# Turning x for layer 1: from TensorE transposes to VectorE blocks of 32 and 16 partition-moving DMAs

## The chip, the cores and the metric

The kernel runs on one core of one Trainium2 chip. The metric is the device time of one execution in microseconds (us); the value given for a kernel is the median of several executions. The profile quoted below comes from one profiled execution of the same program, whose span is 2288.5 us.

## What is computed

The reference puts a batch of 128 graphs, each with 128 nodes and 512 features, through four layers. Every layer adds its result to x and normalises each node's row. Cut to what matters here:

```python
x.shape == (128, 128, 512)                       # float32: graphs b, nodes n, features d
# layer 0
x = layernorm(x + (adj @ x) @ weight + bias)
# layer 1: the layer that the change touches
q, k, v = x @ Wq.T, x @ Wk.T, x @ Wv.T
rel = adj.T * (q @ k.T)                          # 128 x 128 for each graph
rel = rel / norm(rel, axis=2)
x = layernorm(x + rel @ v)
# layer 2: graph attention with softmax, then elu(h' + beta * h)
# layer 3: a maximum over nodes of relu(adj terms), with bias b
```

Layer 1 needs x with its features on the partitions (here called xT), because both the middle product x (Wq' Wk) and the product with Wv sum over features. x as layer 0 leaves it has the nodes on the partitions. Turning it, per graph, is a transpose of 128 nodes by 512 features: four squares of 128 by 128.

## The kernel before

All 128 graphs are taken in 32 groups of G = 4. The four layers of different groups are interleaved: every piece of work has a place in a table, the pieces are sorted by place, and each engine receives its instructions in that order. One group follows another every 28 places. A large product is not done as eight block products but as seven, with sums and differences of the left blocks formed ahead on GpSimd (`left_factors`) and of the results on VectorE and ScalarE (`product`). A half, for the left blocks, is two graphs.

```python
TABLE = dict(
    load=[-20], ..., stats0=row(14.4, 0.4), norm0=[16.2], apply0=row(16.8, 0.33),
    turn=row(21.4, 1), x_sums=row(25.3, 0.5), m=row(28, 1, 7), scores=row(36.5, 1),
    ..., v=row(42, 1, 7), attend=row(50.6, 1), ..., store=[108.5])

def turn(b):                                     # once for each of the 4 graphs of a group
    if b == 0:
        s["xT"] = work.tile([P, K, G * P], FP, tag="aT_x", name=f"xT_{g}")   # one buffer only
    p = bank(f"p_xT_{g}_{b}")                    # a PSUM bank
    for k in range(K):                           # K = 4
        pe.transpose(p[:, k * P : (k + 1) * P], x1[g][:, b, k * P : (k + 1) * P], ident)
    act.copy(s["xT"][:, :, b * P : (b + 1) * P], p.rearrange("p (k n) -> p k n", k=K))

# left_factors: four GpSimd operations that read xT and write s_x
pool.tensor_tensor(s1, blk(1, 0), blk(1, 1), ALU.add)        # and three more of this kind

def by_columns(p, a, b, first):                  # the middle product, r_m: xT or s_x is moving
    for c in range(2):
        for k in range(2):
            pe.matmul(p[:, c, :], b[:, k, c * P : (c + 1) * P], a[:, k, :], ...)

def by_rows(p, a, b, first):                     # the product with Wv, r_v: xT or s_x is stationary
    for j in range(2):
        for k in range(2):
            pe.matmul(p[:, j, :], a[:, k, j * P : (j + 1) * P], b[:, k, :], ...)

def scores(b):                                   # p_rel: xT is stationary
    for k in range(K):
        pe.matmul(s["p"][:, b * P : (b + 1) * P], s["xT"][:, k, b * P : (b + 1) * P],
                  s["tT"][:, k, b * P : (b + 1) * P], ...)
...                                              # (cut)
```

Loads of x and stores of the result are issued from SyncE.

Of the kernel before, what the change touches and what calls it, by code (L numbers as in the profile page):

```python
# [8 lines left out]
FP = mybir.dt.float32  # L9
# [20 lines left out]
def kernel(  # L30
# [31 lines left out]

    nc = tc.nc
    pe, dve, act, pool = (InOrder(tc, e) for e in (nc.tensor, nc.vector, nc.scalar, nc.gpsimd))
    B, N, D = x.shape
    P = 128
    assert N == P and D % P == 0
    K = D // P
    H = D // 2
    G = 4  # L70
    NG = B // G
# [20 lines left out]
    def load(g):  # L92
        x1[g] = data.tile([P, G, D], FP, tag="x1", name=f"x1_{g}", bufs=3)
        if g == 0:
            for b in range(G):
                nc.sync.dma_start(x1[g][:, b, :], x[b])
        else:
            nc.sync.dma_start(x1[g], x[g * G : (g + 1) * G].rearrange("b n d -> n b d"))

    load(0)  # L100
    w0_sb = const.tile([P, K, D], FP)
# [124 lines left out]
    def row(at, step, n=G):  # L226
# [3 lines left out]
    TABLE = dict(  # L230
        load=[-20], y=row(0.5, 1), bias=row(1.3, 1), y_sums=row(5.2, 0.5), y_w=row(7, 1, 7),
        stats0=row(14.4, 0.4), norm0=[16.2], apply0=row(16.8, 0.33),
        turn=row(21.4, 1), x_sums=row(25.3, 0.5), m=row(28, 1, 7), scores=row(36.5, 1),
        masked=[39.95], norms=[42.5], inverse=[43.1], v=row(42, 1, 7), attend=row(50.6, 1),
        residual=row(51.0, 1), dots=row(54.2, 1.1), norm1=[55.2], scale=[58.8],
        apply1=row(65.4, 0.33),
# [5 lines left out]
        stats3=[99.8, 101.1, 104.7, 105.7], norm3=[106.2], apply3=row(107, 0.33), store=[108.5],  # L242
    )

    FIRST = {1: dict(y=row(-9.5, 0.3), bias=row(-9.2, 0.3))}

    LAST = {
        NG - 3: dict(
# [42 lines left out]
    def left_factors(at, s, aT, tag, name, keep):  # L291

        def blk(nh, kh):
            return s[aT][:, 2 * kh : 2 * kh + 2, 2 * P * nh : 2 * P * (nh + 1)]

        def first():
            sums = work.tile([P, 3 + keep, 2, 2 * P], FP, tag=tag, name=f"s_{name}")
            s1, s2, s4 = (sums[:, i] for i in range(3))  # L300
            s3 = sums[:, 3] if keep else blk(1, 0)
            s["f"] = {1: blk(0, 0), 2: blk(0, 1), 3: s4, 4: blk(1, 1), 5: s1, 6: s2, 7: s3}
            pool.tensor_tensor(s1, blk(1, 0), blk(1, 1), ALU.add)

        emit(at[0], first)
        emit(at[1], lambda: pool.tensor_tensor(s["f"][6], s["f"][5], blk(0, 0), ALU.subtract))
        emit(at[2], lambda: pool.tensor_tensor(s["f"][7], blk(0, 0), blk(1, 0), ALU.subtract))
        emit(at[3], lambda: pool.tensor_tensor(s["f"][3], blk(0, 1), s["f"][6], ALU.subtract))

    def by_rows(p, a, b, first):  # L310

        for j in range(2):
            for k in range(2):
                pe.matmul(
                    p[:, j, :],
                    a[:, k, j * P : (j + 1) * P],
                    b[:, k, :],
                    start=(first and j == 0 and k == 0),
                    stop=(j == 1 and k == 1),
                    skip_group_check=True,  # L320
                )

    def by_columns(p, a, b, first):

        for c in range(2):
            for k in range(2):
                pe.matmul(
                    p[:, c, :],
                    b[:, k, c * P : (c + 1) * P],
                    a[:, k, :],  # L330
                    start=(first and c == 0 and k == 0),
                    stop=(c == 1 and k == 1),
                    skip_group_check=True,
                )
# [103 lines left out]
    def layer1(g, t):  # L438
        s = {}

        def turn(b):
            if b == 0:
                s["xT"] = work.tile([P, K, G * P], FP, tag="aT_x", name=f"xT_{g}")
            p = bank(f"p_xT_{g}_{b}")
            for k in range(K):
                pe.transpose(
                    p[:, k * P : (k + 1) * P], x1[g][:, b, k * P : (k + 1) * P], ident
                )
            act.copy(
                s["xT"][:, :, b * P : (b + 1) * P], p.rearrange("p (k n) -> p k n", k=K)  # L450
            )

        def begin_middle():
            s["tT"] = work.tile([P, K, G * P], FP, tag="nat", name=f"tT_{g}", bufs=3)

        def begin_values():
            s["v"] = work.tile([P, G, D], FP, tag="nat", name=f"v_{g}", bufs=3)

        def middle_block(nh, ch):
            return s["tT"][:, 2 * ch : 2 * ch + 2, 2 * P * nh : 2 * P * (nh + 1)]  # L460

        def scores(b):
            if b == 0:
                s["p"] = bank(f"p_rel_{g}")
            for k in range(K):
                pe.matmul(
                    s["p"][:, b * P : (b + 1) * P],
                    s["xT"][:, k, b * P : (b + 1) * P],
                    s["tT"][:, k, b * P : (b + 1) * P],
                    start=(k == 0),  # L470
                    stop=(k == K - 1),
                )

        def masked():
            s["rel"] = work.tile([P, G, P], FP, tag="rel", name=f"rel_{g}", bufs=2)
            dve.tensor_tensor(
                s["rel"], s["p"].rearrange("p (b n) -> p b n", b=G), adj_b, ALU.mult
            )
            s["sq"] = work.tile([P, G, P], FP, tag="sq", name=f"sq_{g}")
            pool.tensor_tensor(s["sq"], s["rel"], s["rel"], ALU.mult)  # L480

        def norms():
            p = bank(f"p_n_{g}")
            for b in range(G):
                pe.matmul(p[:, b : b + 1], s["sq"][:, b, :], ones, start=True, stop=True)
            s["p"] = p

        def inverse():
            n2 = small.tile([P, G], FP, tag="n2", name=f"n2_{g}")
            dve.tensor_copy(n2, s["p"][:, :G])  # L490
            s["rn"] = small.tile([P, G], FP, tag="rn", name=f"rn_{g}")
            pool.tensor_tensor(s["rn"], n2, mhalf, ALU.pow)

        def attend(b):
            s["o", b] = bank(f"p_o1_{g}_{b}")
            pe.matmul(s["o", b], s["rel"][:, b, :], s["v"][:, b, :], start=True, stop=True)

        def residual(b):
            if b == 0:
                x2[g] = data.tile([P, G, D], FP, tag="x2", name=f"x2_{g}")  # L500
            dve.scalar_tensor_tensor(
                x2[g][:, b, :],
                s["o", b],
                s["rn"][:, b : b + 1],
                x1[g][:, b, :],
                op0=ALU.mult,
                op1=ALU.add,
            )
            stats(s, f"1_{g}", b, x2[g][:, b, :])


        def dots(b):
            if b == 0:
                s["d"] = small.tile([P, 2, G], FP, tag="d12", name=f"d12_{g}")
            for i in range(2):
                scr = work.tile([P, D], FP, tag="scr", name=f"scr_{g}_{b}_{i}", bufs=2)
                dve.scalar_tensor_tensor(
                    scr,
                    x2[g][:, b, :],
                    1.0,  # L520
                    wa[:, i, :],
                    op0=ALU.mult,
                    op1=ALU.mult,
                    accum_out=s["d"][:, i, b : b + 1],
                )

        def scale_dots():
            for i in range(2):
                dve.scalar_tensor_tensor(
                    s["d"][:, i, :],  # L530
                    s["mv"][:, :, 0],
                    wa_sum[:, i : i + 1],
                    s["d"][:, i, :],
                    op0=ALU.mult,
                    op1=ALU.add,
                )
            dve.tensor_tensor(
                s["d"], s["d"], s["r", 0][:, None, :].to_broadcast([P, 2, G]), ALU.mult
            )
            s12[g] = s["d"]  # L540

        each(t["turn"], turn)
        left_factors(t["x_sums"], s, "xT", "s_x", f"x_{g}", 1)
        product(t["m"], f"m_{g}", by_columns, s, "m", middle_block, True, begin_middle)
        each(t["scores"], scores)
        emit(t["masked"][0], masked)
        emit(t["norms"][0], norms)
        emit(t["inverse"][0], inverse)
        product(t["v"], f"v_{g}", by_rows, s, "v", rows_of(lambda: s["v"]), True, begin_values)
        each(t["attend"], attend)  # L550
        each(t["residual"], residual)
        each(t["dots"], dots)
        emit(t["scale"][0], scale_dots)
        norm(t["norm1"], t["apply1"], s, f"1_{g}", lambda: x2[g])
# [139 lines left out]
    def layer3(g, t):  # L694
        s = {}
# [12 lines left out]

        def store(i):
            for b in range(i * n, i * n + n):  # L710
                nc.sync.dma_start(out[g * G + b], x3[g][:, b, :])

        n = G // len(t["store"])
        each(t["widen"], widen)
# [46 lines left out]
```

## Time and profile before

| what | value |
|---|---|
| time, median of 3 | 2290.54 us (2290.47 to 2291.78) |
| span of the profiled execution | 2288.5 us |
| granted TensorE clock, mean | 0.996 |
| VectorE (DVE) busy | 1577.0 us, 69% |
| ScalarE (ACT) busy | 1005.3 us, 44% |
| GpSimd (POOL) busy | 959.2 us, 42% |
| moved by DMA in all | 75.21 MB |

How to read the profile: PE is TensorE's matmuls (a transpose is one of them), PEld its weight loads, which run beside matmuls. The names in a group, such as `p_xT<-ident,x`, are the tile that is written and the tiles that are read, in the program's names. Nearly all instructions are recorded at line 26, a helper, so that groups are told apart by tiles and not by lines. The chain of work that ended last is followed back from the last instruction, at each step to what released it or to the instruction ahead of it on its engine.

### The profile page before, as it was taken

The numbers are of one execution on the slowest core, as the hardware profiler recorded it, in microseconds if no ns is written. First come the engines' busy times: TensorE is split into PE (matmuls) and PEld (weight loads), VectorE is DVE, ScalarE is ACT, GpSimd is POOL, SyncE is SP. The second block draws the span as 40 slices with busy tenths as digits, with TensorE's granted clock in tenths as the row PEclk, the third lists the DMA queues.
The fourth block names the chain that finished last, engine by engine and source line by source line (L and its number), as shares of the span: only waits on it lengthen the run. The fifth ranks groups of instructions, "written<-read, shape, count | busy, mean of one in ns | idle before, by whom it ended". The sixth has DMA issues, their size and how long they took to land.

```text
span 2288.5 us, 31182 instructions
## 1 busy us (share of the span) xinstructions
PE 2250.7 (98%) x11809; PEld 1914.8 (84%) x11809; DVE 1577.0 (69%) x3319; ACT 1005.3 (44%) x1800; POOL 959.2 (42%) x775
## 2 busy tenths in 40 slices
PE   7999999999999999999999999999999999999996
PEld 5888888888888888888888888888888888888873
DVE  4656776666776667766667766667767677666677
ACT  2224444444444454444444444444444544444435
POOL 4434444344444334444344443444443344443422
PEclk9999999999999999999999999999999999999998
DMA  4000011100111100111100111001111001110001
GB/s 162 19 19 10 28 38 38 37 21 18 38 37 37 38 19 19 38 37 38 37 10 28 38 37 37 21 18 38 37 37 38 19 20 37 37 38 19 9 12 55
DMA packets 38886, 75.21 MB, mean 33 GB/s; under 512 B 3024, under 2 KB 3152, under 8 KB 38736
## 3 DMA queue, kind: packets, MB, share of 16 engines
q1 hardware_dynamic: 37536, 70.86, 8.7%
q10 hardware_dynamic: 1200, 2.36, 0.3%
q8 instruction: 93, 1.52, 0.3%
q14 instruction: 57, 0.47, 0.1%
HBM read 39.65 MB, written 33.55 MB: 32 GB/s over the span
## 4 chain that ended last, share of the span: by engine, by line
PE 94%; DVE 4%; POOL 1%; ACT 1%; issue 1%; DMA 0%; ACTq 0%; DVEq 0%; POOLq 0%
PE r_y L26 17%; PE r_v L26 16%; PE r_m L26 16%; PE r_z L26 16%; PE p_z L26 5%; PE p_rel L26 5%; PE p_o L26 5%; PE p_a L26 5%; PE p_y L26 5%; PE p_xT L26 2%; DVE x L26 1%; PE p_n L26 1%; DVE st L26 1%; PE p_eT L26 1%; PE p_m L26 1%; PE p_s L26 1%
## 5 line engine op out<-in xcount | busy, mean ns | idle before, releaser
L26 ACT ACTIVATE x<-x,nmean,rstd 128x512 f32<-128x512 f32 x512 | 386.4, 809 | 128.0 <-DVE nmean L26 127.9
L26 DVE BATCH_NORM_STATS2 st<-x 128x6 f32<-128x512 f32 x512 | 352.4, 688 | 75.3 <-ACT x L26 66.6
L26 POOL TENSOR_TENSOR rstd<-ve,mhalf 128x4 f32<-128x4 f32 (+1 forms) x134 | 144.5, 1078 | 245.3 <-DVE ve L26 241.3
L26 POOL TENSOR_TENSOR x<-x,bias_sb 128x512 f32<-128x512 f32 x128 | 174.8, 1368 | 145.5 <-PE p_y L26 145.5
L26 DVE SCALAR_TENSOR_TENSOR scr<-x,wa 128x512 f32<-128x512 f32 x256 | 214.9, 891 | 0.0
L26 ACT ACTIVATE x<-x,top 128x512 f32<-128x512 f32 x128 | 92.4, 722 | 254.1 <-DVE top L26 189.7
L26 DVE TENSOR_TENSOR x<-r_y,x 128x512 f32<-128x512 f32 x224 | 152.9, 683 | 54.4 <-PE r_y L26 44.5
L26 DVE TENSOR_TENSOR v<-r_v,v 128x512 f32<-128x512 f32 x96 | 65.8, 685 | 177.0 <-PE r_v L26 174.0
L26 POOL TENSOR_TENSOR s_x<-xT 128x512 f32<-128x512 f32 x64 | 82.2, 1285 | 222.2 <-ACT xT L26 222.2
L26 ACT COPY yT<-p_y 128x512 f32<-128x512 f32 x128 | 75.0, 586 | 206.0 <-PE p_y L26 206.0
L26 DVE SCALAR_TENSOR_TENSOR x<-p_o,rn,x 128x512 f32<-128x512 f32 x128 | 95.9, 749 | 99.5 <-PE p_o L26 96.5
L26 DVE SCALAR_TENSOR_TENSOR x<-m,x 128x512 f32<-128x512 f32 x128 | 115.1, 899 | 61.7 <-ACT m L26 51.3
L26 ACT COPY c<-r_z 128x512 f32<-128x512 f32 x124 | 72.6, 585 | 175.9 <-DVE scr L26 151.5
L26 PEld LDWEIGHTS p_y<-adjT,x 128*128 128x128 f32 x1024 | 135.3, 194 | 12.9 <-ACT adjT L26 5.0
L26 PEld LDWEIGHTS p_z<-eT,x 128*128 128x128 f32 x1024 | 135.4, 194 | 8.3 <-DVE x L26 1.2
L26 PE MATMUL p_y<-adjT,x 128*128 128x128 f32 x1024 | 136.1, 278 | 6.2 <-ACT adjT L26 4.7
L26 PEld LDWEIGHTS p_rel<-tT,xT 128*128 128x128 f32 x1024 | 134.2, 192 | 7.4 <-DVE tT L26 0.8
L26 PE MATMUL p_a<-x,adjT 128*128 128x512 f32 x256 | 133.6, 607 | 3.5 <-DVE mx L26 1.8
L26 PE MATMUL p_z<-eT,x 128*128 128x128 f32 x1024 | 136.4, 277 | 0.4 <-DVE x L26 0.4
L26 PE MATMUL p_rel<-tT,xT 128*128 128x128 f32 x1024 | 135.0, 275 | 0.6 <-DVE tT L26 0.6
L26 POOL TENSOR_TENSOR s_z<-zT 128x512 f32<-128x512 f32 x31 | 39.2, 1265 | 223.9 <-ACT zT L26 223.9
L26 PE MATMUL p_o<-v,rel 128*128 128x512 f32 x256 | 130.6, 594 | 0.0
(120 smaller groups left out, 5075.2 us busy)
## 6 DMA issues: line engine op xcount, KB each, us to landing
out_dram<-x SPq DMA_DIRECT2D x128, 256.0 KB, 2.0
x<-in_x_dram SPq DMA_DIRECT2D x31, 1024.0 KB, 5.2
w_sb<-in_L_gnn_weight_dram ACTq DMA_DIRECT2D x1, 1024.0 KB, 5.7
x<-in_x_dram SPq DMA_DIRECT2D x4, 256.0 KB, 7.5
wq_sb<-in_L_gnn_Wq_dram SPq DMA_DIRECT2D x1, 1024.0 KB, 11.7
wk_sb<-in_L_gnn_Wk_dram SPq DMA_DIRECT2D x1, 1024.0 KB, 14.6
w_sb<-in_L_gnn_W_dram ACTq DMA_DIRECT2D x1, 1024.0 KB, 10.2
wv_sb<-in_L_gnn_Wv_dram SPq DMA_DIRECT2D x1, 1024.0 KB, 13.7
```

What stands on the lines that cost most here:

```text
L26: return lambda *args, **kw: self.tc.keep_in_program_order(op(*args, **kw))
```

## The change

The transposes of x for layer 1 leave TensorE, and the copies out of PSUM leave ScalarE, for every group but the first. VectorE turns x in square blocks of 32 by 32 (one instruction for each graph). A block so turned lies on the 32 partitions from which it was read, so 16 DMAs for each group, issued from SyncE, then carry the blocks between the four sets of 32 partitions: one DMA for each pair of source set a and destination set q. Each carries 32 partitions by 8 runs by 64 elements of 4 bytes: 64 KB in runs of 256 bytes. So that a run is 256 bytes long and not 128, the columns of the two graphs of a half are interleaved: even columns belong to one, odd columns to the other. Matmuls that read xT or s_x as one graph therefore read every second element. The purpose is to give TensorE's time for the transposes to matmuls. Loads and stores on SyncE are now recorded in program order with the new DMAs.

```diff
@@ the table @@
-        turn=row(21.4, 1), x_sums=row(25.3, 0.5), m=row(28, 1, 7), scores=row(36.5, 1),
+        turn=row(18.4, 0.6), move=row(20.5, 0.1), x_sums=row(25.3, 0.5), m=row(28, 1, 7), scores=row(36.5, 1),
@@ columns of the two graphs of a half @@
+    def graphs(a, mixed):
+        if mixed:
+            return a.rearrange("p k (n j) -> p k j n", j=2)
+        return a.rearrange("p k (j n) -> p k j n", j=2)
@@ by_rows, for v alone with mixed=True @@
-                    a[:, k, j * P : (j + 1) * P],
+                    graphs(a, mixed)[:, k, j, :],
@@ by_columns @@
-                    p[:, c, :],
+                    p[:, c, :].rearrange("p (j n) -> p j n", j=2),
                     b[:, k, c * P : (c + 1) * P],
-                    a[:, k, :],
+                    graphs(a, True)[:, k, :, :],
@@ layer 1 @@
         def turn(b):
             if b == 0:
-                s["xT"] = work.tile([P, K, G * P], FP, tag="aT_x", name=f"xT_{g}")
-            p = bank(f"p_xT_{g}_{b}")
...
+                s["xB"] = work.tile([P, 2, K, Q, 2 * P // Q], FP, tag="xB", name=f"xB_{g}")
+                s["xT"] = work.tile([P, 2, K, 2 * P], FP, tag="aT_x", name=f"xT_{g}")
+            if g == 0:
...                                  (the first group: as before, with the columns interleaved)
+                return
+            dve.transpose(
+                s["xB"][:, b // 2].rearrange("p k q (u j) -> p (k q) u j", j=2)[:, :, :, b % 2],
+                x1[g][:, b, :].rearrange("p (c u) -> p c u", u=P // Q),
+            )
+
+        def move(a):
+            n = P // Q
+            for q in range(Q):
+                sync.dma_start(
+                    s["xT"][q * n : (q + 1) * n, :, :, 2 * a * n : 2 * (a + 1) * n].rearrange(
+                        "p h k n -> p (h k) n"
+                    ),
+                    s["xB"][a * n : (a + 1) * n, :, :, q, :].rearrange("p h k n -> p (h k) n"),
+                )
@@ scores @@
-                    s["xT"][:, k, b * P : (b + 1) * P],
+                    graphs(s["xT"][:, b // 2], True)[:, k, b % 2, :],
@@ the pieces of layer 1 @@
         each(t["turn"], turn)
+        if g > 0:
+            each(t["move"], move)
```

More of the change, by code (lines that the diff above doesn't have):

```diff
@@ L64 @@
     pe, dve, act, pool = (InOrder(tc, e) for e in (nc.tensor, nc.vector, nc.scalar, nc.gpsimd))
+    sync = InOrder(tc, nc.sync)
     B, N, D = x.shape
@@ L68 @@
     K = D // P
+    Q = P // 32
     H = D // 2
@@ L97, in load @@
         else:
-            nc.sync.dma_start(x1[g], x[g * G : (g + 1) * G].rearrange("b n d -> n b d"))
+            sync.dma_start(x1[g], x[g * G : (g + 1) * G].rearrange("b n d -> n b d"))
     load(0)
@@ L243 @@
     )
-    FIRST = {1: dict(y=row(-9.5, 0.3), bias=row(-9.2, 0.3))}
+    FIRST = {
+        0: dict(turn=row(20.4, 0.3)),
+        1: dict(y=row(-9.5, 0.3), bias=row(-9.2, 0.3))}
     LAST = {
@@ L295, in blk @@
         def blk(nh, kh):
+            if keep:
+                return s[aT][:, nh, 2 * kh : 2 * kh + 2, :]
             return s[aT][:, 2 * kh : 2 * kh + 2, 2 * P * nh : 2 * P * (nh + 1)]
@@ L308, in left_factors, with by_rows @@
         emit(at[3], lambda: pool.tensor_tensor(s["f"][3], blk(0, 1), s["f"][6], ALU.subtract))
-    def by_rows(p, a, b, first):
+    def graphs(a, mixed):
+        if mixed:
+            return a.rearrange("p k (n j) -> p k j n", j=2)
+        return a.rearrange("p k (j n) -> p k j n", j=2)
+    def by_rows(p, a, b, first, mixed=False):
         for j in range(2):
@@ L321, in by_rows, with by_mixed_rows @@
                 )
+    def by_mixed_rows(p, a, b, first):
+        by_rows(p, a, b, first, mixed=True)
     def by_columns(p, a, b, first):
@@ L442, in turn @@
             if b == 0:
-                s["xT"] = work.tile([P, K, G * P], FP, tag="aT_x", name=f"xT_{g}")
-            p = bank(f"p_xT_{g}_{b}")
-            for k in range(K):
-                pe.transpose(
-                    p[:, k * P : (k + 1) * P], x1[g][:, b, k * P : (k + 1) * P], ident
-                )
-            act.copy(
-                s["xT"][:, :, b * P : (b + 1) * P], p.rearrange("p (k n) -> p k n", k=K)
-            )
+                s["xB"] = work.tile([P, 2, K, Q, 2 * P // Q], FP, tag="xB", name=f"xB_{g}")
+                s["xT"] = work.tile([P, 2, K, 2 * P], FP, tag="aT_x", name=f"xT_{g}")
+            if g == 0:
+                p = bank(f"p_xT_{g}_{b}")
+                for k in range(K):
+                    pe.transpose(
+                        p[:, k * P : (k + 1) * P], x1[g][:, b, k * P : (k + 1) * P], ident
+                    )
+                act.copy(
+                    graphs(s["xT"][:, b // 2], True)[:, :, b % 2, :],
+                    p.rearrange("p (k n) -> p k n", k=K),
+                )
+                return
+            dve.transpose(
+                s["xB"][:, b // 2].rearrange("p k q (u j) -> p (k q) u j", j=2)[:, :, :, b % 2],
+                x1[g][:, b, :].rearrange("p (c u) -> p c u", u=P // Q),
+            )
+        def move(a):
[7 more added lines that the diff above has]
+                )
         def begin_middle():
@@ L548, in layer1 @@
         emit(t["inverse"][0], inverse)
-        product(t["v"], f"v_{g}", by_rows, s, "v", rows_of(lambda: s["v"]), True, begin_values)
+        product(t["v"], f"v_{g}", by_mixed_rows, s, "v", rows_of(lambda: s["v"]), True, begin_values)
         each(t["attend"], attend)
@@ L710, in store @@
             for b in range(i * n, i * n + n):
-                nc.sync.dma_start(out[g * G + b], x3[g][:, b, :])
+                sync.dma_start(out[g * G + b], x3[g][:, b, :])
         n = G // len(t["store"])
```

## The prediction

> **What bounds the kernel now.** I read the busy shares first, then the chain of work that ended last, then that chain inside one group, and last the waits and DMA issues around xT. The page's first part and the head of its chain:
>
> ```profile
> PE 2250.7 (98%) x11809; PEld 1914.8 (84%) x11809; DVE 1577.0 (69%) x3319; ACT 1005.3 (44%) x1800; POOL 959.2 (42%) x775
> ...
> PE 94%; DVE 4%; POOL 1%; ACT 1%; issue 1%; DMA 0%; ACTq 0%; DVEq 0%; POOLq 0%
> PE r_y L26 17%; PE r_v L26 16%; PE r_m L26 16%; PE r_z L26 16%; PE p_z L26 5%; PE p_rel L26 5%; PE p_o L26 5%; PE p_a L26 5%; PE p_y L26 5%; PE p_xT L26 2%; DVE x L26 1%; PE p_n L26 1%; DVE st L26 1%; PE p_eT L26 1%; PE p_m L26 1%; PE p_s L26 1%
> ```
>
> TensorE is busy 98% of the span and is 94% of the chain. A busy PE alone proves little, but its idle time is at most 2288.5 - 2250.7 = 38 us in all, so time can only be gained by giving it less to do. The transposes of x, p_xT, stand in the chain with 2%. What one costs there is read from the chain in one group's stretch (start, length, what):
>
> ```profile
> 1051.75 1.73 PE r_v L26 x8
> 1053.47 0.86 PE p_a L26 x2
> 1054.33 1.73 PE r_z L26 x8
> 1056.06 0.44 PE p_xT L26 x4
> 1056.49 1.73 PE r_z L26 x8
> 1058.22 0.44 PE p_xT L26 x4
> ...
> 1071.61 1.73 PE r_m L26 x8
> ```
>
> Pieces stand end to end without a gap, and the four transposes of a graph take 0.44 us of it. The group table says 273 ns for one such matmul, but they overlap; the 0.44 is what they hold up. The busy time of stretches of 4 us (stretch, its length, then busy PE, PEld, DVE, ACT and POOL) gives the room beside them:
>
> ```profile
> 1044.00:1048.00 4.00, 4.00 (x24) 3.64 (x23) 0.51 (x2) 4.00 (x8) 0.00 (x0) 1.00 0.00 0
> 1048.00:1052.00 4.00, 4.00 (x22) 3.26 (x21) 1.60 (x3) 1.40 (x3) 2.06 (x2) 1.00 0.00 0
> 1052.00:1056.00 4.00, 4.00 (x18) 3.10 (x17) 2.36 (x6) 1.80 (x3) 2.93 (x3) 1.00 0.02 4
> ```
>
> Here, where the change puts VectorE's transposes, TensorE is full and VectorE nearly free. Groups that give sizes for the new work, one wait, and the DMA issues:
>
> ```profile
> L26 PE MATMUL p_xT<-ident,x 128*128 128x128 f32 x512 | 76.2, 273 | 0.0
> L26 ACT COPY xT<-p_xT 128x512 f32<-128x512 f32 x128 | 74.5, 586 | 95.4 <-PE p_xT L26 95.3
> L26 DVE TENSOR_TENSOR x<-r_y,x 128x512 f32<-128x512 f32 x224 | 152.9, 683 | 54.4 <-PE r_y L26 44.5 <-POOL x L26 6.9 <-DVE nmean L26 0.3
> ```
>
> ```profile
> POOL s_x L26 <- ACT xT L26: 222.2, 31, 10.9
> ```
>
> ```profile
> out_dram<-x SPq DMA_DIRECT2D x128, 256.0 KB, 2.0
> x<-in_x_dram SPq DMA_DIRECT2D x31, 1024.0 KB, 5.2
> ```
>
> GpSimd waits 222 us for xT without holding anybody up, so xT may come somewhat earlier or later. A 256 KB store lands 2.0 us after its issue.
>
> [...]
>
> **Removed.** For 31 groups, 4 graphs each, four transposes on TensorE: 1.75 us a group (5.0% of the 35 us of the chain's stretch; 4 x 0.44). All of it lies in the full stretch of TensorE, so 31 x 1.75 = 54 us leave the path. ScalarE loses 124 copies of 0.586 us = 73 us, worth nothing on the path. Group 0 keeps its transposes.
>
> **Added on VectorE.** 124 transposes, estimated at 0.69 us from the 683 ns of a 128x512 operation: 86 us, which brings VectorE to 1663 us, 74% of a span of 2236. The built order puts them among the additions of r_v, at 1046 to 1053 in the time of the group above. Between 1044 and 1052 VectorE is busy 2.1 of 8 us, so 4 x 0.69 = 2.8 us fit. ScalarE's normalisation of x for the fourth graph ends near 1049, so the inputs are there, and the last transpose, behind the maximum of a p_a in the order, ends near 1053. Nothing on the path.
>
> **Added on the DMA queues.** 16 moves of 64 KB a group, 31 x 16 = 496 in all, 32.5 MB of 256-byte runs. xT has one buffer, so the first move waits for the last reader of the group ahead, the r_v piece that ends at 1053.47. From there to the first r_m at 1071.61 are 18.1 us, and 18.1 - 1.75 = 16.4 us after the change. A SyncE issue takes 0.33 us for a store and 0.39 us for a load in the trace's timeline. I choose 0.4: 16 x 0.4 = 6.4 us, and 2.0 us to land, so xT is whole 8.4 us after 1053.47, some 8 us before TensorE wants it. GpSimd needs 2 x 1.28 = 2.6 us for the first two sums, which TensorE wants at its third r_m step, 5.2 us into the product. That is in time too; xT even comes near 1062, earlier than the 1065 of the trace. [...]
>
> **Moved.** Stores of an older group now stand behind the moves in the queue and go out some us later; the next load, 8 us behind them, has most of a group's 69 us to spare. On TensorE the order is the old one without p_xT, and without the p_xT banks the p_o and p_y tiles turn over the four PSUM banks with fewer pieces between. VectorE reads a p_o within some 1.6 us, so a bank is free in time.
>
> **Sum.** 2290.5 - 54 = 2236; I add 1 us for small waits at the group borders and say 2237.
>
> **Rivals.** (1) *Strided operands.* All seven steps of r_m stream every second element, and the weight loads of r_v and p_rel read so. If strided reading were slower by only a tenth on r_m, 7 x 1.73 x 0.1 = 1.2 us a group, or 37 us, would go back, and the time would be near 2273. Weight loads have less room: a r_v load takes 190 ns beside a matmul that holds TensorE 216 ns (1.73/8). [...] for it nothing in the trace. (2) *The moves become the wait.* If one cost over 16.4/16 = 1.0 us, TensorE would wait at each r_m. At 1.2 us, 16 x 1.2 + 1 = 20.2 us, a wait of 3.8 us takes the place of 1.75 saved: 31 x 2 us more, near 2355. The trace's issues of 0.3 to 0.4 us and its 2.0 us landings speak against it[...]. (3) *VectorE.* From 1068 to 1076 it is busy 7.8 of 8 us; TensorE now gets there 1.75 us sooner a group. If VectorE's additions came late there, up to half of the gain is lost, near 2263. Against it: by the same view it is idle for 6.3 of the 16 us ahead of 1068, so it reaches that stretch sooner too.
>
> **Range and chances.** The gain of 54 us is the firmest number, and nothing in the profile can make it larger than the small waits that vanish with it, so the low end is close: 2230. The high end, 2275, holds the strided rival at a tenth and the VectorE rival. To be faster by over 2% the time must be under 2245, that is, only 9 us of the 54, 0.3 us a group, may be lost. I give 0.69 to faster, 0.23 to within 2% (rivals 1 and 3), and 0.08 to slower (rival 2).
>
> **What would show it.** Right: no p_xT in the chain beyond group 0; groups 67.7 us apart instead of 69.5; r_m pieces still 1.73 us and r_v loads still near 190 ns; a transpose on VectorE near 0.7 us; xT landed some 8 us ahead of the first r_m; TensorE's busy time down by about 54 us with idle time still near 38 us. Wrong: longer r_m, r_v or p_rel pieces (rival 1); TensorE waiting on a DMA for xT (rival 2); TensorE waiting on VectorE for tT, c or x (rival 3).

## The result and the profile after

| | time, median | runs |
|---|---|---|
| before | 2291.16 us | 2290.47 to 2291.84 |
| after | 2276.24 us | 2274.21 to 2276.67 |

The ratio is 0.9933, with a 95% interval of 0.9916 to 0.995. The change gains 15 us where the prediction had 54; the time lies just above the range of 2230 to 2275. The profile of after, busy time and the head of the chain of work that ended last:

```profile
PE 2226.3 (98%) x11313; PEld 1879.1 (83%) x11313; DVE 1763.1 (78%) x3443; ACT 939.2 (41%) x1676; POOL 1011.9 (44%) x775
...
PE 91%; DVE 5%; POOL 1%; issue 1%; ACT 1%; DMA 0%; SPq 0%; ACTq 0%; DVEq 0%; POOLq 0%
PE r_y L26 17%; PE r_v L26 16%; PE r_m L26 16%; PE r_z L26 16%; PE p_rel L26 5%; PE p_z L26 5%; PE p_o L26 5%; PE p_a L26 5%; PE p_y L26 4%; DVE x L26 1%; DVE scr L26 1%; PE p_n L26 1%; DVE st L26 1%; PE p_eT L26 1%; PE p_m L26 1%
```

p_xT has left the chain, as meant. But TensorE's busy time fell by 24 us and not by 54, and idle time rose from 38 to 48 us (2274.3 - 2226.3): TensorE does its remaining work more slowly, and waits more. VectorE's busy time grew by 186 us, of which the new transposes are only 84. In the names, r_y and r_z are the large products of layers 0 and 2, p_o is rel @ v, p_s and p_eT are small transposes of layer 2, and scr are VectorE's dot products of x with the attention weights of layer 2. The chain of after through the stretch shown in the prediction, and on to the product r_y:

```profile
1052.35 1.73 PE r_v L26 x8
...
1067.00 3.45 PE r_z L26 x16
1070.46 1.81 PE r_m L26 x8
1072.27 0.89 PE p_y L26 x8
...
1090.59 0.93 PE p_rel L26 x8
1091.52 1.96 PE r_y L26 x8
```

The last two pieces had these lengths before:

```profile
1091.16 0.89 PE p_rel L26 x8
1092.05 1.73 PE r_y L26 x8
```

A step of r_v still takes 1.73 us and p_y 0.89. A step of r_m now takes 1.81 instead of 1.73, and the p_rel of a graph 0.93 instead of 0.89. The r_y behind it takes 1.96 where nothing in it is strided: 0.23 us of that is a wait.

To say where all of the time went I took from the trace, for every TensorE matmul, the time from its start to the start of the next one, and added these up by the tile written. A wait counts with the piece ahead of it. The differences from before, in us:

| | p_xT | r_m | p_rel | p_o | p_s and p_eT | r_y | rest | sum |
|---|---|---|---|---|---|---|---|---|
| after | -54.1 | +18.5 | +7.1 | +8.8 | +5.2 | +1.7 | -1.4 | -14.2 |

So the 54 us were gained, and 40 us were given back: 41.3 in the columns from r_m to r_y, less 1.4 in the rest. A typical r_m matmul starts its successor after 227 ns instead of 216, a p_rel matmul after 118 instead of 112. The +8.8 at p_o is one wait, in group 1, from the list of TensorE's waits:

```profile
PE r_m L26 <- DMA xT<-xB: 8.8, 1, 8.8
```

The rest are small waits on VectorE, and most groups have none. Between the first r_m matmuls of groups 2 to 31 there are 29 distances. In after 21 of them are 68.47 or 68.48 us; the other eight are 69.04 to 70.61, together 9.4 us longer. In seven of the eight, GpSimd's first sum of xT starts only 2.0 to 3.1 us ahead of the first r_m matmul, because one of the 16 copies was issued or landed later than usual (why is not shown); in the 21 it starts 3.2 to 4.1 us ahead. The eighth follows two of the seven, and it is the one in the chain above.

Four reasons were to be tested, with the letters that the expectations use. A: the strided reading of xT and s_x slows TensorE by itself. B: the moves or VectorE's transposes slow r_m. C: xT is whole later than foreseen, so that GpSimd's sums of xT fall beside VectorE's operations and both are slowed. D: VectorE's 124 added transposes make it late by their own time. D is the rival of C, since both make TensorE wait on VectorE. Group 1's wait was to be removed by itself.

What speaks for C: the queue of SyncE in one group, and then GpSimd (the first line is before, the others after) and VectorE (after) beside the start of r_m (start, length, what; in brackets the idle time ahead of it and what ended it).

```profile
1054.14 10.40 SPq L26 DMA_DIRECT2D xT<-xB  x16
1064.64 2.01 SPq L26 DMA_DIRECT2D out_dram<-x  x4
```

```profile
1065.41 1.28 POOL L26 TENSOR_TENSOR s_x<-xT 128x512 f32<-128x512 f32 x1 [7.00 <-ACT xT L26]
...
1066.41 1.27 POOL L26 TENSOR_TENSOR s_x<-xT 128x512 f32<-128x512 f32 x1 [7.39 <-PE r_z L26]
...
1070.66 1.73 POOL L26 TENSOR_TENSOR s_x<-xT,s_x 128x512 f32<-128x512 f32 x1
```

```profile
1068.66 0.92 DVE L26 SCALAR_TENSOR_TENSOR scr<-x,wa 128x512 f32<-128x512 f32 x1
...
1069.51 1.75 DVE L26 SCALAR_TENSOR_TENSOR scr<-x,wa 128x512 f32<-128x512 f32 x1
...
1072.34 0.68 DVE L26 SCALAR_TENSOR_TENSOR scr<-x,wa 128x512 f32<-128x512 f32 x1
```

The group of scr, before and then after:

```profile
L26 DVE SCALAR_TENSOR_TENSOR scr<-x,wa 128x512 f32<-128x512 f32 x256 | 214.9, 891 | 0.0
L26 DVE SCALAR_TENSOR_TENSOR scr<-x,wa 128x512 f32<-128x512 f32 x256 | 274.6, 1124 | 0.0
```

Sixteen issues take 10.4 us, 0.65 from one to the next (median of an issue alone 0.61), and with 2.1 us to land xT is whole 12.3 us after its last reader. GpSimd's first sum shows the moment: 1066.41 (the bracket names PE r_z, but the last of the 16 copies lands at 1066.08, just ahead of it). That is 4.05 us ahead of the first r_m at 1070.46. Before the change it was 6.20 us ahead (1065.41 and 1071.61). The four sums therefore end 1.9 us after r_m begins instead of 1.1 us before, and lie beside VectorE's scr operations. One of these takes 0.68 us with no sum beside it and 1.75 beside one; the sum takes 1.73 instead of 1.27. Over the whole trace 111 of the 256 scr operations take more than 1 us, against 65 before: 51 lie beside a sum (31 before) and 58 beside the additions of the bias that GpSimd does after the sums (32 before). Of VectorE's 186 us more, 60 are scr's and 84 the transposes.

### The profile page after: what moved, and what is told of

It is laid out like the page before. It is cut to its first block, busy times and chain, and to the rows that moved or that the text cites. A ratio compares the mean times of both kernels' runs of the same rounds, so it can differ in the third digit from the quotient of the medians.

```text
span 2274.3 us, 31117 instructions
## 1 busy us (share of the span) xinstructions
PE 2226.3 (98%) x11313; PEld 1879.1 (83%) x11313; DVE 1763.1 (78%) x3443; ACT 939.2 (41%) x1676; POOL 1011.9 (44%) x775
## 4 chain that ended last, share of the span: by engine, by line
PE 91%; DVE 5%; POOL 1%; issue 1%; ACT 1%; DMA 0%; SPq 0%; ACTq 0%; DVEq 0%; POOLq 0%
PE r_y L26 17%; PE r_v L26 16%; PE r_m L26 16%; PE r_z L26 16%; PE p_rel L26 5%; PE p_z L26 5%; PE p_o L26 5%; PE p_a L26 5%; PE p_y L26 4%; DVE x L26 1%; DVE scr L26 1%; PE p_n L26 1%; DVE st L26 1%; PE p_eT L26 1%; PE p_m L26 1%
## 5 line engine op out<-in xcount | busy, mean ns | idle before, releaser
L26 DVE SCALAR_TENSOR_TENSOR scr<-x,wa 128x512 f32<-128x512 f32 x256 | 274.6, 1124 | 0.0
L26 POOL TENSOR_TENSOR x<-x,bias_sb 128x512 f32<-128x512 f32 x128 | 192.9, 1513 | 99.2 <-PE p_y L26 99.1
L26 POOL TENSOR_TENSOR s_x<-xT 128x512 f32<-128x512 f32 x64 | 95.7, 1495 | 253.6 <-PE r_z L26 124.5
L26 PEld LDWEIGHTS p_rel<-tT,xT 128*128 128x128 f32 x1024 | 140.3, 196 | 6.3 <-DVE tT L26 0.6
L26 PE MATMUL p_rel<-tT,xT 128*128 128x128 f32 x1024 | 140.3, 280 | 0.4 <-DVE tT L26 0.4
L26 PE MATMUL r_m<-xT,m_qk 128*128 128x256 f32 x512 | 127.8, 392 | 8.8 <-DMA xT<-xB 8.8
L26 DVE SCALAR_TENSOR_TENSOR x<-m,x 128x512 f32<-128x512 f32 x128 | 123.2, 963 | 13.5 <-DVE x L26 0.5
L26 ACT COPY tT<-r_m 128x512 f32<-128x512 f32 x128 | 75.5, 590 | 132.9 <-PE r_m L26 132.9
```

What stands on the lines that cost most here:

```text
L26: return lambda *args, **kw: self.tc.keep_in_program_order(op(*args, **kw))
```

## Experiments

### The stride by itself: interleave_only and unmix_at_eviction

The first keeps the turn on TensorE for all groups and only interleaves the columns: no VectorE transposes, no moves.

```diff
-            if g == 0:
+            if True:                       # all groups turned by TensorE, columns interleaved
...
-        if g > 0:
-            each(t["move"], move)
```

> The kernel before with the columns of two graphs interleaved and nothing else: TensorE still transposes x, no VectorE transposes, no moves. Theory A (reading every second column costs TensorE time by itself): r_m pieces of 8 go from 1.73 to 1.81 us and p_rel from 0.89 to 0.93 us as in the changed kernel, so 32 x (7 x 0.08 + 4 x 0.04) = 23 us are added to 2290.5: about 2314. Theory B (r_m is slower because the moves or VectorE's transposes disturb it): 1.73 us a piece and about 2291.

Measured: 2313.48 us, ratio 1.01 (1.0085 to 1.0116). Its chain:

```profile
1083.15 1.81 PE r_m L26 x8
...
1103.29 0.93 PE p_rel L26 x8
```

In the accounting r_m is at +18.6 and p_rel at +5.0, all other columns are within 0.2, and the sum is +23.3 us. r_m is as long as in after although nothing moves and VectorE turns nothing, so B falls. Stride alone costs 23 us.

The second keeps the whole change, but the middle product streams the columns as they lie, and its result is put in order by the engines that read it out of PSUM.

```diff
 by_columns:
-                    p[:, c, :].rearrange("p (j n) -> p j n", j=2),
+                    p[:, c, :],
-                    graphs(a, True)[:, k, :, :],
+                    a[:, k, :],
 where the product leaves PSUM:
+            if mul is by_columns:
+                p = p.rearrange("p c (n j) -> p c j n", j=2)
+                dst = dst.rearrange("p c (j n) -> p c j n", j=2)
```

> The changed kernel, but the middle product streams its 256 columns in the order in which they lie, and the two graphs are told apart when ScalarE and VectorE read the result out of PSUM. p_rel and r_v keep their strided weight loads. Theory A: r_m pieces back at 1.73 us, so 32 x 7 x 0.08 = 18 us less than 2276: about 2258, with p_rel still 0.93. Theory B: r_m stays at 1.81 and the time at 2276. If reading PSUM with a stride is slow, the copies and additions of tT (590 and 677 ns before) get longer and part of the gain is lost.

Measured: 2264.02 us, ratio 0.9879 (0.986 to 0.9899). A typical r_m matmul is back at 216 ns, and r_m at +1.0 us instead of +18.5. Reading every second element of PSUM costs ScalarE and VectorE nothing that shows (tT<-r_m 591 and 675 ns, against 590 and 675 in after). But of 17.5 us only 9.3 in this accounting reach the end: p_s and p_eT rise from +5.2 to +9.2 and p_rel from +7.1 to +9.0. (The medians of after and of this run lie 12 us apart; this profiled execution, 2266.68 us, is among the longer of four from 2259.35 to 2267.83.) I take it that a faster r_m leaves VectorE less time for its part, so that its lateness shows more; this run does not test that by itself.

### How far a stride may go: strides_alone

The kernel before, with 16 more matmuls of each of ten kinds on data at rest, at its end (the 320 of the expectation are their passes); their results are not used. mv streams 256 elements: one row contiguous, both rows of an interleaved pair, one row of every second element, a pair interleaved in blocks of 32, every fourth, every eighth. st loads weights at stride 1, 2, 4 and 8 and streams 64 elements, so that the load is the bound.

```diff
+    for name, a in streams.items():
+        for _ in range(16):
+            pe.matmul(d, adjT, a, start=True, stop=True)
+    for name, b in loads.items():
+        for _ in range(16):
+            pe.matmul(p[:, :64], b, flat[:, :64], start=True, stop=True)
```

> The kernel before with 320 matmuls (of float32, two passes each, adjT or a slice of the layer 2 weights as operands, results unused) behind its last one: six patterns of 256 streamed columns with a contiguous stationary operand, then four strides of a stationary operand of 128 columns with 64 columns streamed, which leaves the weight load the bound. Cost of each element at a stride: a pass of 256 columns at stride 2 takes 227 ns whether in two rows or one, against 216 contiguous and 216 in blocks of 32; a load at stride 2 takes about 6 ns more than a contiguous one. Cost of each row of the pattern: one row at stride 2 takes 216 to 221 ns, eight blocks of 32 about 250. Strides 4 and 8 tell whether it grows.

The chain names each kind. Such a float32 matmul is recorded as two passes, so x32 is 16 matmuls.

```profile
2284.71 7.25 PE mvpair L26 x32
2291.96 7.25 PE mvtwo L26 x32
2299.22 6.91 PE mvblock L26 x32
2306.12 14.50 PE mvfour L26 x32
2320.62 14.76 PE mveight L26 x32
2335.38 3.52 PE stone L26 x32
2338.90 3.77 PE sttwo L26 x32
2342.67 7.51 PE stfour L26 x32
2350.18 7.64 PE steight L26 x32
```

Divided by 32: a pass over 256 streamed elements takes 216 ns in blocks of 32, 227 at stride 2 (in one row or in two, so it is a cost of the element and not of the row), 453 at stride 4, 461 at stride 8. A bound weight load takes 110, 118, 235 and 239, with the same 64 elements streamed each time. The contiguous row (mvone, not shown, since its piece holds a wait) also starts a pass every 216 ns in the median. Stride 2 costs 5 to 7%, and stride 4 doubles the time.

### Group 1's wait: group1_on_tensor

TensorE turns group 1 as well as group 0.

```diff
-        1: dict(y=row(-9.5, 0.3), bias=row(-9.2, 0.3))}
+        1: dict(y=row(-9.5, 0.3), bias=row(-9.2, 0.3), turn=row(21.4, 1))}
-            if g == 0:
+            if g <= 1:
-        if g > 0:
+        if g > 1:
```

> The changed kernel with the first two groups on TensorE in place of the first alone. The trace shows TensorE waiting 8.8 us for the first moves, because in group 1 only four p_o pieces lie between the last reader of xT and the first r_m. If that wait is lost time: 9.0 us come back and 1.75 us of transposes are paid, so about 2269. If the wait only hides another that takes its place (weights for layer 2, the first elu): about 2276.

Measured: 2271.21 us, ratio 0.9917 (0.9903 to 0.9932). The wait of 8.8 us is gone, 1.8 us of p_xT are back; small waits on VectorE rise by some 4 us (p_s and p_eT from 5.2 to 7.5, r_m and p_rel by 1.7), so that less than 7 us are gained: 3 in the accounting, whose execution is the longest of the four, and 5 in the medians. So that wait was lost time. In group 1 only four p_o stood between the last reader of xT and the first r_m, because the older groups whose work fills this place do not exist yet.

### No stride at all: contiguous_128B

The columns of a graph lie together again, and a move carries 512 runs of 128 bytes instead of 256 of 256.

```diff
-            return a.rearrange("p k (n j) -> p k j n", j=2)
+            return a.rearrange("p k (j n) -> p k j n", j=2)
-                s["xB"] = work.tile([P, 2, K, Q, 2 * P // Q], FP, tag="xB", name=f"xB_{g}")
+                s["xB"] = work.tile([P, 2, K, 2, Q, P // Q], FP, tag="xB", name=f"xB_{g}")
 in move:
-                    s["xB"][a * n : (a + 1) * n, :, :, q, :].rearrange("p h k n -> p (h k) n"),
+                    s["xB"][a * n : (a + 1) * n, :, :, :, q, :].rearrange("p h k j n -> p (h k j) n"),
```

> The changed kernel without interleaving: each graph has its own columns, and the 16 moves carry 512 runs of 128 bytes each in place of 256 runs of 256 bytes. Theory A: r_m at 1.73 and p_rel at 0.89 us, 23 us less: about 2253 if a move still takes SyncE about 0.6 us (a cost of each DMA). If the 0.6 us is a cost of each run, a move takes 1.2 us, 16 take 19 us and land 21 us after the last reader of xT, where TensorE has room for 16.4: about 5 us of waiting in each of 30 groups, near 2400.

Measured: 2282.74 us, ratio 0.9967 (0.9957 to 0.9978): slower than after, although r_m and p_rel matmuls are back at 216 and 112 ns. The head of its chain tells why:

```profile
PE 65%; DVE 28%; issue 4%; POOL 1%; ACT 1%; DMA 0%; SPq 0%; DVEq 0%; ACTq 0%; POOLq 0%
```

VectorE has risen from 5% of the chain to 28%. In the accounting p_rel is at +15.1, p_s and p_eT at +17.8 and r_y at +6.6, all of it waits (the profiled execution, 2287.41 us, is the longest of eight, so at the median they are some 5 us less). The shorter runs themselves cost little: the issue takes 628 ns against 608 (medians) and the copy lands in 2.3 us against 2.1, half a us in all 16. But xT is whole only 3.3 us ahead of the first r_m (1073.63 and 1076.95), and scr operations take 1183 ns in the mean against 1124 in after. From group 2 on the first sum is never more than 3.4 us ahead of the first r_m matmul, and TensorE waits for VectorE in every group. Taking the stride away alone uncovered waits larger than what it saved.

### VectorE's own work or its collisions: unused_vector_turns and moves_two_queues

The first is the kernel before, with the 124 transposes of VectorE at the places that the change gives them; nothing reads their result.

```diff
+            dve.transpose(
+                s["xB"][:, b // 2].rearrange("p k q (u j) -> p (k q) u j", j=2)[:, :, :, b % 2],
+                x1[g][:, b, :].rearrange("p (c u) -> p c u", u=32),
+            )
+        if g > 0:
+            each([28.0 * g + 18.4 + 0.6 * b for b in range(G)], turn_unused)
```

> The kernel before plus VectorE's 124 transposes into a tile that nobody reads; TensorE still makes xT. This measures VectorE's added work alone (0.70 us each, 87 us in all). Theory C: they lie in idle time and the time stays at 2291, with scr still near 891 ns. Theory D: VectorE's operations after them come late and TensorE waits: 2300 or more.

Measured: 2290.72 us, ratio 0.9999 (0.999 to 1.0007). VectorE is busy 1655.8 us, and TensorE waits for it no more than before. D finds no support at the old pace of TensorE; the next run has the same transposes at the new one.

The second is after, with six of the 16 moves issued from ScalarE, so that xT is whole sooner.

```diff
-        def move(a):
+        def move(a, queue=sync, qs=range(Q)):
...
-            each(t["move"], move)
+            for a in (0, 1):
+                emit(t["move"][a], move, a)
+            emit(t["move"][2], lambda: move(2, sync, (0, 1)))
+            emit(t["move"][3] + 1.0, lambda: move(2, act, (2, 3)))
+            emit(t["move"][3] + 1.0, lambda: move(3, act))
```

> The changed kernel with 10 of a group's 16 moves issued from SyncE and 6 from ScalarE, so that xT is whole about 3.5 us sooner (10 x 0.61 + 2.1 = 8.2 us after its last reader, or the ScalarE ones at 9, in place of 12.2). Theory C (GpSimd's sums of xT now fall on VectorE's two-input operations, both take longer, and VectorE is late for TensorE): with earlier sums the scr operation falls from 1124 ns back toward 891, VectorE's busy time from 1763 toward 1700 us, and the small waits of TensorE on VectorE, some 5 us, go; the wait of group 1 shrinks from 9 to about 5 us. About 2267 in place of 2276. Theory D (VectorE is late because it has 2.8 us more work a group): VectorE's waits stay, only group 1 gains: about 2272.

Measured: 2265.89 us, ratio 0.9891 (0.9876 to 0.9906). Its busy times, and the group of scr:

```profile
PE 2221.2 (98%) x11313; PEld 1876.9 (83%) x11313; DVE 1663.9 (74%) x3443; ACT 935.8 (41%) x1676; POOL 963.7 (43%) x775
...
L26 DVE SCALAR_TENSOR_TENSOR scr<-x,wa 128x512 f32<-128x512 f32 x256 | 204.2, 849 | 0.0
```

xT is now whole 6.4 us ahead of r_m (1055.65 and 1062.07). VectorE is busy 99 us less for the same instructions, and p_s and p_eT drop from +5.2 to -0.3, r_y from +1.7 to +0.2, p_rel to +5.3, which is the stride; of p_o's +6.4, 5.2 us are what is left of group 1's wait. All 124 transposes are still on VectorE. C holds and D falls: it was when xT came, not what VectorE had to do.

### Putting it together

contiguous_two_queues_g1 joins three edits shown above: no interleaving, groups 0 and 1 on TensorE, and moves from two queues.

> No interleaving (runs of 128 bytes), moves on two queues, the first two groups turned by TensorE. In the run without interleaving r_m and p_rel were back at 1.73 and 0.89 us, but TensorE waited some 29 us more for VectorE. Theory C: with the sums earlier those waits go, and with group 1's wait gone the whole gain comes in: 2290.5 - 30 x 1.75 = 2238, plus some 5 to 10 us of waits left: 2243 to 2248. Theory D: the waits stay and the time is near 2275.

Measured: 2250.03 us, ratio 0.9819 (0.9803 to 0.9836). The waits on VectorE are gone (p_rel 0.0, p_s and p_eT +0.5), although scr takes 1112 ns in the mean, nearly as much as in after. So the collisions alone cost TensorE nothing. They did where xT was late: here the first sum starts 4.3 to 5.7 us ahead of the first r_m matmul from group 2 on. But p_o shows +7.8. In 29 of 30 groups an r_z matmul behind a p_o starts late; where the list of waits names what it waited for, that is ScalarE's copy c<-r_z (3.3 us in five waits). ScalarE, held by six issues (4.49 us in one group), came late to it.

Two kernels shift ScalarE's part ahead of that copy, one with six moves, one with four:

```diff
-            emit(t["move"][3] + 1.0, lambda: move(2, act, (2, 3)))
-            emit(t["move"][3] + 1.0, lambda: move(3, act))
+            emit(t["move"][3] + 0.05, lambda: move(2, act, (2, 3)))    # with four: on sync instead
+            emit(t["move"][3] + 0.05, lambda: move(3, act))
```

> As contiguous_two_queues_g1 (2250.03 us), but ScalarE issues its six moves about one place (2.5 us) earlier, ahead of a copy of r_z's result that there came late. That run lost 7.8 us on waits of r_z for a tile that ScalarE writes. If those waits came from the place of the issues, they go, and the time is 2242 us: 2290.5 less 30 groups of 1.75 us is 2238, and I leave 4 us for small waits. If ScalarE's issues delay some other copy wherever they stand, the time stays near 2250 us and the waits of r_z for zT stay near 8 us or move to another product.

Measured: 2283.33 us, ratio 0.9962 (0.9947 to 0.9977). That was worse than either thing expected. ScalarE's timeline and TensorE's waits:

```profile
1051.96 4.65 ACTq L26 DMA_DIRECT2D xT<-xB  x6
1056.74 0.72 ACT L26 ACTIVATE x<-x,top 128x512 f32<-128x512 f32 x1 [4.50 <-DMA xT<-xB]
1057.36 0.57 ACT L26 COPY c<-r_z 128x512 f32<-128x512 f32 x1
```

```profile
PE r_z L26 <- ACT c L26: 39.5, 31, 1.7
```

The six issues hold ScalarE for 4.65 us, and now they stand ahead of a copy that TensorE needs in every group: 1.3 us of waiting in each of 30 groups (of the 31 waits, before has one, of 1.1 us).

> As contiguous_6_on_scalar_early, with 12 moves on SyncE and 4 on ScalarE. ScalarE is held some 1.2 us less in a group, and xT is whole some 1.2 us later (12 issues of 0.61 us instead of 10). If ScalarE's lateness is what costs, this is the faster of the two by a few us, about 2240 us; if the sums of GpSimd, which start when xT is whole, and VectorE's operations beside them are what costs, it is slower by a few us, about 2247 us, with a longer mean of scr<-x,wa.

Measured: 2236.53 us (2235.61 to 2236.92), ratio 0.9756 (0.974 to 0.9773). Four issues take 2.84 us, and the copy comes in time. Busy times, head of the chain and a group of it:

```profile
PE 2197.1 (98%) x11329; PEld 1866.0 (83%) x11329; DVE 1676.9 (75%) x3439; ACT 937.1 (42%) x1680; POOL 982.3 (44%) x775
...
PE 94%; DVE 3%; POOL 1%; ACT 1%; issue 0%; DMA 0%; ACTq 0%; DVEq 0%; POOLq 0%
```

```profile
1048.41 1.73 PE r_m L26 x8
...
1067.96 0.89 PE p_rel L26 x8
1068.86 1.73 PE r_y L26 x8
```

Every piece is at its old length, and TensorE's idle time is 38 us again, as before. xT is whole 5.6 us ahead of r_m. With 988 ns scr is still longer than before (891), and no wait follows from it. The accounting side by side, against before:

| | p_xT | r_m | p_rel | p_o | p_s and p_eT | r_y | rest | sum |
|---|---|---|---|---|---|---|---|---|
| contiguous_128B | -54.1 | +1.6 | +15.1 | +9.4 | +17.8 | +6.6 | +0.9 | -2.8 |
| moves_two_queues | -54.1 | +18.2 | +5.3 | +6.4 | -0.3 | +0.2 | -1.3 | -25.5 |
| contiguous_two_queues_g1 | -52.4 | +1.5 | 0.0 | +7.8 | +0.5 | +0.1 | +2.5 | -40.0 |
| contiguous_6_on_scalar_early | -52.4 | +1.3 | -0.6 | +43.1 | +0.3 | -0.2 | +2.1 | -6.4 |
| contiguous_4_on_scalar_early | -52.4 | +1.1 | -0.6 | -0.2 | +0.2 | -0.2 | -1.7 | -53.8 |

contiguous_4_on_scalar_early beats both kernels, before and after, by some 55 us and 40 us. It is the gain that the change was to bring, with its three costs taken away.

## Why the prediction was wrong, by its steps

- **Removed: 54 us.** Right. The accounting gives 54.1, and contiguous_4_on_scalar_early, at a sum of -53.8, shows that a gain of this size can reach the end.
- **Added on VectorE: 86 us, nothing on the path.** Right for the transposes: 84.0 us, 700 ns each, and unused_vector_turns shows that they cost nothing. The total of 1663 us is what moves_two_queues has (1663.9); after has 1763.1, and 60 of these 100 us more are scr operations that take longer than before.
- **The stride.** This is the step that failed first: the sum of 2237 counts nothing for the interleaved columns. That was an assumption of mine; nothing in the trace before shows what a strided operand costs. The runs gave 5% on r_m and p_rel (216 to 227 ns and 112 to 118), 23.5 us of the 40 that were given back. A step of r_m took 1.81 us instead of 1.73. Rival 1 had the mechanism. Its tenth on r_m was twice too much (37 us for a measured 18.6); p_rel's weight loads, named there without a number, added 5.0 us. The r_v loads, named there too, stayed hidden: r_v's steps kept 1.73 us, though a load took 196 ns there instead of 190.
- **Added on the DMA queues: 16 x 0.4 + 2.0 = 8.4 us.** This failed too. The landing was right (2.1), the issue was not: 10.4 us for 16 instead of 6.4. I took the issue of a store or a load and there was no row for a copy within SBUF. xT came 4 us ahead of r_m instead of 8. Rival 2 in its main form stayed away, since 0.65 is below the 1.0 us that it needs.
- **Which group.** The room of 16.4 us was read from a group in the middle. Group 1 has no such room and waited 8.8 us, once. This was overlooked altogether.
- **GpSimd "in time", and "xT may come somewhat earlier or later".** The sums were in time for TensorE, as said, but the step asked only who waits for them and not what runs beside them. Four us later than foreseen, more of them met VectorE's scr operations, and in the eight groups named above VectorE came late for TensorE. This is rival 3's loss by another cause: 9 us, counting p_s, p_eT, r_y and the part of p_rel that is not stride (5.2 + 1.7 + 2.1).
- **Sum.** 2237 + 23.5 (stride) + 8.8 (group 1) + 9.0 (VectorE), less 1.4 of the rest and the 1 us allowed for small waits, is 2276, which is what was measured; the terms come from the accounting of the trace, so they must close. Groups stand 68.47 us apart in the median of after, some of them 70.6; in contiguous_4_on_scalar_early 67.70, the spacing predicted.

What stays open: the 39 us of waits on VectorE in the accounting of contiguous_128B vanish with an earlier xT and group 1 on TensorE, but how much each collision puts on TensorE was not separated. A layout with blocks of 32 columns, which the stream reads for nothing (216 ns) and which would keep runs of 256 bytes, was not tried: the weight loads of r_v and p_rel would have to read such blocks too, and no run here loads weights so.

## What to carry to other kernels

When a saving on the bound engine is paid for with a new access pattern, measure the pattern on that engine first: a handful of matmuls at the end of the kernel tells it in one run. Issue time holds an engine (here 0.61 us of SyncE for one copy, 4.65 us of ScalarE for six), so count it by a row of the same kind of copy, spread it over queues, and look what stands behind it in each. And for work that comes later than before, ask not only who waits for it but also what it now runs beside.

## What the runs showed of the hardware

- TensorE with float32 operands: a stride of 2 elements costs 5% on the stream (216 to 227 ns for 256) and 7% on a load that is the bound (110 to 118), 4 elements double both (453, 235), and 8 add little more (461, 239). Blocks of 32 contiguous elements took 216 ns, as a contiguous row does.
- A copy of 64 KB from 32 partitions to 32 others holds SyncE for 0.61 us with runs of 256 bytes and 0.63 with twice as many of 128, against 0.39 for a load of 1 MB in the same trace. Twice the runs added 0.02 us. In the two early versions, where ScalarE and SyncE issue from the same moment on, one copy took 0.71 us of ScalarE with four of them (2.84) and 0.78 with six (4.65), and landed 3.1 to 3.6 us after its issue instead of 2.1 (after) or 2.3 (contiguous_128B). In moves_two_queues ScalarE's six took 4.24 us, 0.71 each, and a copy landed after 2.2 to 2.3 us. From the first issue of a group to the end of the last, two queues took 7.46, 8.03, 8.46 and 9.29 us (one group of each of four kernels) instead of 10.4.
- A 128x512 float32 transpose in blocks of 32 takes VectorE 700 ns, about what an addition of that size takes (683).
- Reading PSUM at every second float32 cost neither VectorE nor ScalarE anything that shows: 675 and 591 ns, against 675 and 590 contiguous.
